# Which PSUM bank the score products for the row maxima of a causal attention use, and in which order they come

## The chip, the cores and the metric

One Trainium2 chip, of which the kernel uses one core. Times are device microseconds (us) of that core. TensorE is called PE, its weight loads PEld, VectorE DVE, ScalarE ACT, GpSimd POOL, SyncE SP, as in the profile. A bank is one eighth of the core's PSUM, as wide as 512 float32 numbers on each of 128 partitions; the kernel holds one matmul result in one.

## The reference

A diffusion transformer block with adaptive layer norm, in float32, for x of 2 x 2048 x 512 and a condition of 2 x 512:

```python
mod = silu(condition) @ Wada + bada
sh_a, sc_a, gt_a, sh_m, sc_m, gt_m = split(mod, 6)
xm = layernorm(x, g1, be1) * (1 + sc_a) + sh_a
x = x + gt_a * attention(xm, Wqkv, Wproj, bproj)   # 16 heads of 32, causal softmax
xm = layernorm(x, g2, be2) * (1 + sc_m) + sh_m
x = x + gt_m * (gelu(xm @ W1 + b1) @ W2 + b2)      # 512 -> 2048 -> 512
```

The part that matters is `attention`: for each head, scores of 2048 queries with the keys up to their own place, softmax over the keys, and the weighted sum of the values. The softmax subtracts each query's largest score, so this maximum has to be known before the exponentials are taken.

## The kernel before, in words

**Stages.** QKV of batch 0 (to 209 us), attention of batch 0 (209 to 741), projection and QKV of batch 1 (to 981), attention of batch 1 (981 to 1516), projection and the MLP (to the end, 2338). The attention of both batches runs the same program with the same order.

**Units and steps.** A unit (`units`) is a group c of 4 heads and a block i of 512 queries: 16 units in a batch, u0 to u15, with i in the order 0, 1, 2, 3 for the first group and 0, 2, 1, 3 for the others. A unit has 4i + 3 steps (`steps_of`): 4i + 1 with a full tile of 128 keys against 512 queries, then a step with two tiles of the diagonal (384 + 128 wide) and one with the last tile (256 wide). A batch has 144 steps; steps are numbered here through the batch.

**One step** (`scores_t`). Four banks `st` are taken from a pool of four. PE first writes the negative row maxima into each, as a product of `fold` with `sel`; then, for each of four heads, the scores are added (`st<-qst,kst`). ACT takes the exponential into `e` (L630); on the diagonal POOL zeroes what lies above it (`affine_select`, L636). POOL adds the exponentials of four steps into `ee` (L658; DVE does so in the last unit). Two steps later PE multiplies the exponentials with the values (`o`) and the sums with ones (`sm`).

**The maxima of later units** are found beside this, with the same scores computed a second time, the other way round (queries on partitions): "score products", `s<-kst,qst` in the trace. Their list is `Row.todo`, filled by `banks_of`: an item fills one bank, and is a unit, a key block and one or two parts (head, row tile). For a key block before the diagonal an item is a *single*: 128 queries against 512 keys, without a mask. In the diagonal block a row tile t needs only 128(t + 1) keys; tiles of 128 and 384, or of 256 and 256, go together as a *pair* in one bank, and the tile of 512 is a masked single. A unit has 6 pairs and 4 + 16i singles, 10 + 16i banks; a batch 544. `bank` issues the products and, for each part, DVE's maximum: `tensor_reduce` (L500) without a mask, and with a mask a custom operation that writes `junk`, with a read of its accumulator (both L495).

After a unit's last item, `split` (L503 to L521: operations at L517, L518, L519, L520 and L521) writes the maximum as three bfloat16 pieces into `mhl`; two of its intermediate results lie in the PSUM bank of that last item. Later `rows` transposes `mhl` on PE (`ps_m`) and DVE builds `fold` from it (L565).

**Banks.** PSUM's eight banks in the attention: `st` four, `o` and `sm` one each, and `s` two, for score products and for `ps_m`. One score product of each step with three or more of them borrows an st bank (`st_bank`), so such a step takes five banks from the pool of four: the fourth `fold` product of the next step goes into the bank in which the borrowed score product was. In the last unit, the fifth and sixth of every six st allocations go to the s pool instead.

**Order.** `count` and `due` decide how many items a step issues (n, by costs, so that each unit's maxima are ready some steps ahead). Within a step their places are fixed: one after the first head, one after the second, both in s banks; at the end a third in the borrowed bank and a fourth in an s bank, before the `o` products of an earlier step. Items are taken strictly in the list's order. PE, ACT and POOL run in the program's order; DVE's maxima, splits and folds are placed by a scheduler. During QKV, `tick` calls `score` for the first three units, without borrowing.

Of the kernel before, what the change touches and what calls it, by code (L numbers as in the profile page):

```python
# [27 lines left out]
def dit_block_kernel(  # L28
# [42 lines left out]
    HC = P // HD  # L71
# [63 lines left out]
    first = const.tile([P, 1], F32, tag="first", name="first")  # L135
# [68 lines left out]
    def mm(*args, **kw):  # L204

        return tc.keep_in_program_order(nc.tensor.matmul(*args, **kw))  # L206

    def act(ins):

        return tc.keep_in_program_order(ins)  # L210
# [84 lines left out]
    class Row:  # L295
# [234 lines left out]
                n += 1  # L530
            return n

        def score(self, n, borrow=None):

            for k in range(n):
                if borrow and k % 2 == 0:
                    s = borrow()  # L540
                else:
                    s = ps_sp.tile([P, QB], F32, tag="s", name="s")
                item = self.todo.pop(0)
                u = item[0]
                if self.mx is None:
                    self.mx = bp.tile(
                        [P, HC * TQ, units[u][1] + 1], F32, tag="mx", name="mx", bufs=3
                    )
                self.bank(*item, s)
                if not self.todo or self.todo[0][0] != u:  # L550
                    self.split(u, self.mx, s)
                    self.mx = None
                    self.at += 1
# [26 lines left out]
    def attention_phase(row):  # L580
        b, vv, kst, qst = row.b, row.vv, row.kst, row.qst
        with pool(f"att{b}") as ap, pool(
# [6 lines left out]
            def scores_t(u, step, n):  # L589

                def st_bank():

                    n_bank[0] += u == len(units) - 1
                    if n_bank[0] % 6 >= HC:
                        return ps_sp.tile([P, QB], F32, tag="s", name="st")
                    return ps_stp.tile([P, QB], F32, tag="st", name="st")

                c, i = units[u]
                tiles = steps_of[u][step]
                q0 = tiles[0][1]
                w = sum(QB - q for _, q in tiles)
                sts, es = [], []  # L610
                for h in range(HC):
                    g = slice(h * HD, (h + 1) * HD)
                    st = st_bank()
                    mm(
                        st[:, :w], sel[g, :], fold[u % 2][g, q0 : q0 + w],
                        start=True, stop=False,
                    )
                    sts.append(st)
                for h in range(HC):
                    at = 0  # L620
                    for j, q in tiles:
                        mm(
                            sts[h][:, at : at + QB - q],
                            kst[c, j // TQ][:, h, j % TQ * P : (j % TQ + 1) * P],
                            qst[u][:, h, q:],
                            start=False, stop=at + QB - q == w,
                        )
                        at += QB - q
                    e = ap.tile([P, QB], F32, tag="e", name="e", bufs=E_BUFS)
                    act(nc.scalar.activation(e[:, :w], sts[h][:, :w], AF.Exp))  # L630
                    if tiles[0][0] >= i * TQ:

                        d = e.rearrange("p (t k) -> p t k", k=P)[:, 0 : TQ : TQ - 1, :]
                        d = d[:, : len(tiles), :]
                        act(
                            nc.gpsimd.affine_select(  # L636
                                d, d, pattern=[[0, len(tiles)], [1, P]],
                                compare_op=ALU.is_ge, fill=0.0,
                                base=0, channel_multiplier=-1,
                            )  # L640
                        )
                    es.append(e)
                    if h < 2 and n >= 3 or h >= HC - n and n < 3:
                        row.score(1)
                if n >= 3:
                    row.score(1, st_bank)
                    row.score(min(n, HC) - 3)
                return es, max(0, n - HC)

            def new_sums():  # L650
# [59 lines left out]
            def due(u, step):  # L710

                rate, past = 0.0, weight[step]
                for v in range(u + 1, len(units)):

                    left = sum(weight[step : max(step + 1, starts[v] - 3)])
                    rate = max(rate, (cum[v] - row.spent) / left)
                return row.spent + rate * past

            for u, (c, i) in enumerate(units):
# [5 lines left out]
                for n_step, tiles in enumerate(steps_of[u]):  # L725
                    last = n_step == steps - 1
                    if n_step == 0:
# [5 lines left out]
                    n = row.count(  # L733
                        due(u, starts[u] + n_step) - QB // 2,
                        u + AHEAD - (n_step < 2 and u > 0),
                    )
                    if u == 0 and n_step < LAG:

                        n = max(n, HC)
                    es, rest = scores_t(u, n_step, n)  # L740
                    rest = len(row.todo) - rest
                    make_rows = False
# [37 lines left out]
                    if n_step < i * TQ:  # L780
                        k = n_step % TQ
# [492 lines left out]
    row = Row(0)  # L1274
# [167 lines left out]
    past, row = row, Row(1)  # L1442
# [594 lines left out]
```

## Time and profile before

| | |
|---|---|
| median of 3 runs | 2343.66 us (2343.58 to 2346.75) |
| profiled execution | 2339.57 us, span 2337.8, granted clock 0.997 |
| POOL's additions (L658, into a running sum) | 424 of 1293 ns |
| exponentials (L630) | 1152 of 578 ns |
| score products in s banks / in st banks (matmuls) | 994 / 286 |
| full-width maxima from s / from st banks (L500) | 608 / 160 |
| splits in s / in st banks | 24 / 8 |

The table counts operations in the whole program, with both batches. A row of the profile names engine, line, operation and `out<-in` tiles with the shape; the times in a timeline row are start and duration, and in brackets stands how long the engine was idle ahead of it and what released it. PE's matmuls are pipelined: their starts are recorded, their ends are modelled, so that rows overlap.

### The profile page before, as it was taken

The page shows a single profiled execution, that of the slowest core. Times are in us where ns is not written, and L with a number is a line of the kernel's source. Part 1 is how long each engine was busy: PE and PEld are TensorE (multiplying, and loading weights), DVE is VectorE, ACT ScalarE, POOL GpSimd, SP SyncE. Part 2 cuts the span into 40 slices and gives each one's busy share as a digit, 9 for nine tenths or more (in the row PEclk, how much of TensorE's full clock was granted, in tenths as well). Part 3 has the DMA queues.
Part 4 walks back from the last instruction along what each step waited for, and adds up shares of the span by engine and source line. Part 5 has one row for each costly group of instructions (what it writes and reads, how often), then busy time and mean ns, then how long its engine had stood idle before and what let it go on. Part 6 is the DMA issues. An engine that isn't in the chain of part 4 may idle for free.

```text
span 2337.8 us, 34364 instructions
## 1 busy us (share of the span) xinstructions
PE 2272.5 (97%) x12033; PEld 1376.1 (59%) x12033; DVE 1432.3 (61%) x3025; ACT 1007.9 (43%) x1952; POOL 1119.2 (48%) x1261
## 2 busy tenths in 40 slices
PE   7999999999999999999999999999999999999998
PEld 5787445455544588754545554344585486487477
DVE  4677766767657657777576766562473383375356
ACT  4434555555555243355555555603323322332320
POOL 7153997988893692289888898450000000000000
PEclk9999999999999999999999999999999999999999
DMA  9887132231223796622324113263354254353433
GB/s 303 272 277 185 33 86 65 64 83 46 91 100 116 260 307 222 167 60 67 75 64 100 42 42 133 97 229 108 107 176 154 84 176 145 116 162 126 141 120 131
DMA packets 160518, 311.64 MB, mean 133 GB/s; under 512 B 16544, under 2 KB 48844, under 8 KB 158552
## 3 DMA queue, kind: packets, MB, share of 16 engines
q1 hardware_dynamic: 155488, 285.53, 40.5%
q0 software_dynamic: 4480, 23.36, 2.6%
q8 instruction: 95, 1.56, 0.3%
q14 instruction: 79, 0.65, 0.1%
q10 hardware_dynamic: 376, 0.55, 0.1%
HBM read 229.95 MB, written 87.29 MB: 136 GB/s over the span
## 4 chain that ended last, share of the span: by engine, by line
PE 83%; DVE 6%; POOL 6%; issue 2%; DMA 2%; ACT 1%; SPq 0%; DVEq 0%; POOLq 0%; ACTq 0%
PE ps_a L206 24%; PE st L206 15%; PE ps_b L206 12%; PE o L206 9%; PE s L206 7%; PE ps_c L206 6%; POOL ee L658 5%; PE sm L206 4%; PE ps_o L206 3%; DVE junk L495 2%; PE ps_xt L214 1%; DVE mx L500 1%; POOL e L636 1%; ACT e L630 1%; PE ps_o L214 1%
## 5 line engine op out<-in xcount | busy, mean ns | idle before, releaser
L630 ACT ACTIVATE e<-st 128x512 f32<-128x512 f32 (+1 forms) x1152 | 574.5, 578 | 413.6 <-PE st L206 380.0
L500 DVE TENSOR_REDUCE mx<-s 128x1 f32<-128x512 f32 x608 | 406.2, 686 | 223.1 <-PE s L206 221.8
L658 POOL TENSOR_TENSOR ee<-ee,e 128x512 f32<-128x512 f32 x424 | 529.1, 1293 | 3.5 <-ACT e L630 3.3
L206 PE MATMUL st<-qst,kst 128*128 128x512 f32 (+3 forms) x1280 | 410.6, 386 | 0.0
L206 PE MATMUL s<-kst,qst 128*128 128x512 f32 (+3 forms) x994 | 375.3, 402 | 6.0 <-DVE mx L500 3.1
L206 PE MATMUL ps_a<-sum,w 128*128 128x256 f32 (+1 forms) x1088 | 346.6, 454 | 0.0
L206 PE MATMUL o<-e,vv 128*32 128x512 f32 (+3 forms) x2560 | 310.2, 539 | 6.9 <-POOL e L636 6.7
L206 PEld LDWEIGHTS st<-qst,kst 128*128 128x128 f32 x1280 | 227.8, 188 | 117.6 <-issue 88.3
L206 PEld LDWEIGHTS ps_a<-sum,w 128*128 128x128 f32 x1088 | 206.4, 190 | 109.7 <-issue 91.3
L658 POOL TENSOR_TENSOR ee<-e 128x512 f32<-128x512 f32 x168 | 210.3, 1288 | 102.3 <-ACT e L630 100.6
L495 DVE CUSTOM_DVE_ANT_0 junk<-s,causal 128x128 bf16<-128x128 f32 (+3 forms) x386 | 188.5, 488 | 92.4 <-PE s L206 85.0
L206 PEld LDWEIGHTS s<-kst,qst 128*128 128x128 f32 x994 | 185.7, 188 | 55.5 <-DVE mx L500 20.5
L636 POOL TENSOR_SCALAR_AFFINE_SELECT e<-e 128x128 f32<-128x128 f32 (+1 forms) x384 | 123.6, 362 | 73.1 <-ACT e L630 70.8
L206 PEld LDWEIGHTS <-sel 32*128 32x128 bf16 x1152 | 29.5, 91 | 199.7 <-issue 199.7
L1616 DVE TENSOR_TENSOR h<-c,ps_b 128x512 f32<-128x512 f32 x32 | 22.0, 688 | 202.0 <-PE ps_b L206 202.0
L206 PE MATMUL st<-fold,sel 32*128 32x512 bf16 (+1 forms) x1152 | 127.9, 372 | 13.5 <-DVE mx L495 6.4
L206 PEld LDWEIGHTS o<-e,vv 128*32 128x32 f32 x2560 | 65.3, 108 | 112.4 <-issue 72.8
L1790 ACT ACTIVATE h<-h,cols 128x512 f32<-128x512 f32 x96 | 69.3, 722 | 120.5 <-DVE h L1616 120.5
L206 PE MATMUL ps_b<-sum,w 128*128 128x256 f32 (+1 forms) x384 | 120.6, 450 | 0.0
L500 DVE TENSOR_REDUCE mx<-st 128x1 f32<-128x512 f32 x160 | 109.4, 684 | 2.4 <-PE st L206 0.6
L985 POOL TENSOR_TENSOR lo<-lo,hi 128x512 fp32r<-128x512 f32 x32 | 40.7, 1274 | 130.4 <-ACT hi L983 124.1
L206 PE MATMUL st<-kst,qst 128*128 128x512 f32 (+3 forms) x286 | 98.0, 370 | 0.0
(210 smaller groups left out, 3113.9 us busy)
## 6 DMA issues: line engine op xcount, KB each, us to landing
kst<-k SPq DMA_DIRECT2D x128, 256.0 KB
qst<-q SPq DMA_DIRECT2D x128, 256.0 KB
w<-w1d SPq DMA_DIRECT2D x32, 896.0 KB
w<-w2d SPq DMA_DIRECT2D x28, 1024.0 KB
w<-w2d SPq DMA_DIRECT2D x28, 768.0 KB
q<-hi SPq DMA_DIRECT2D x32, 256.0 KB
q<-lo SPq DMA_DIRECT2D x32, 256.0 KB
k<-hi SPq DMA_DIRECT2D x32, 256.0 KB
```

Source lines behind the costliest of these rows:

```text
L206: return tc.keep_in_program_order(nc.tensor.matmul(*args, **kw))
L214: return tc.keep_in_program_order(nc.tensor.transpose(dst, src, ident[:n, :n]))
L495: nc.vector.tensor_tensor_reduce(junk[:, :w], x, causal[:, QB - w :], 1.0, MASKED, ALU.add, ALU.max, m,)
L500: nc.vector.tensor_reduce(m, x, axis=AX.X, op=ALU.max)
L630: act(nc.scalar.activation(e[:, :w], sts[h][:, :w], AF.Exp))
L636: nc.gpsimd.affine_select(d, d, pattern=[[0, len(tiles)], [1, P]], compare_op=ALU.is_ge, fill=0.0, base=0, channel_multiplier=-1,)
L658: act(engine.tensor_tensor(dst, x, y, ALU.add))
L985: engine.tensor_tensor(lo, d, hi.bitcast(F32), ALU.subtract)
L1616: act(nc.vector.tensor_tensor(dst, x, y, ALU.add))
L1790: nc.scalar.activation(d, ps, AF.Gelu, bias=col(r_b1 + half * HF + f, 1))
```

## The change

`score` gets a third argument, and looks ahead over the first eight items of the list that belong to the unit whose turn it is. Items with two parts are `pairs`, the others `singles`. The borrowed bank is taken only if a single is among them and the unit's last item isn't the only one left (the item after which `split` runs in the item's bank); else the product goes to an s bank. The item taken is the first single of those ahead, and for the call at the end of a step (`late=True`) the first pair; where there is none of the kind, the first item. The order within a unit thus changes; which items belong to which unit does not, nor how many a step issues, but for the costs that `count` finds in the items that are left.

```diff
-        def score(self, n, borrow=None):
+        def score(self, n, borrow=None, late=False):
             for k in range(n):
-                if borrow and k % 2 == 0:
+                u = self.todo[0][0]
+                ahead = [j for j, item in enumerate(self.todo[:8]) if item[0] == u]
+                pairs = [j for j in ahead if len(self.todo[j][2]) > 1]
+                singles = [j for j in ahead if j not in pairs]
+                lent = borrow and singles and len(ahead) > 1
+                if lent:
                     s = borrow()
                 else:
                     s = ps_sp.tile([P, QB], F32, tag="s", name="s")
-                item = self.todo.pop(0)
-                u = item[0]
+                first = pairs if late else singles
+                item = self.todo.pop((first or [0])[0])
...
                 if n >= 3:
                     row.score(1, st_bank)
-                    row.score(min(n, HC) - 3)
+                    row.score(min(n, HC) - 3, late=True)
```

The calls during QKV (`late` not given) take singles first too. After the change, lines behind L533 stand five lines further down.

## The prediction

> **What bounds the kernel now.** First the page: which engine is busy, and which engines stand on the chain that ends last.
>
> ```profile
> PE 2272.5 (97%) x12033; PEld 1376.1 (59%) x12033; DVE 1432.3 (61%) x3025; ACT 1007.9 (43%) x1952; POOL 1119.2 (48%) x1261
> PE 83%; DVE 6%; POOL 6%; issue 2%; DMA 2%; ACT 1%; SPq 0%; DVEq 0%; POOLq 0%; ACTq 0%
> ```
>
> TensorE (PE) is the bound, and the change leaves it the same matmuls. So only time in which PE is held can be won or lost. Next, the waits of PE over the whole span (us in total, times, longest), as far as they end on buffers of the attention:
>
> ```profile
> PE o L206 <- POOL e L636: 6.7, 10, 1.2
> PE st L206 <- DVE mx L495: 6.4, 12, 0.8
> PE st L206 <- DVE mhl L521: 6.2, 8, 1.1
> PE s L206 <- DVE mx L500: 3.1, 6, 1.1
> PE s L206 <- DVE mhl L521: 1.8, 4, 0.6
> ```
>
> The second and third rows are what the diff can touch first. A step opens with four `st<-fold` products into the four st banks; the borrowed bank makes a fifth allocation in a step, so the fourth fold product of the next step waits until VectorE (DVE) has read the borrowed bank. The timeline of PE shows five such steps, an unheld one (407.03), and an s product that waits for a split (276.81):
>
> ```profile
> 265.04 0.39 PE L206 MATMUL st<-fold,sel 32*128 32x512 bf16 x3
> 266.14 0.37 PE L206 MATMUL st<-fold,sel 32*128 32x512 bf16 x1 [0.70 <-DVE mx L495]
> ...
> 276.81 0.50 PE L206 MATMUL s<-kst,qst 128*128 128x512 f32 x1 [0.62 <-DVE mhl L521]
> ...
> 289.29 0.65 PE L206 MATMUL st<-fold,sel 32*128 32x512 bf16 x4
> ...
> 407.03 0.40 PE L206 MATMUL st<-fold,sel 32*128 32x512 bf16 x4
> ...
> 410.45 0.39 PE L206 MATMUL st<-fold,sel 32*128 32x512 bf16 x3
> 411.65 0.37 PE L206 MATMUL st<-fold,sel 32*128 32x512 bf16 x1 [0.81 <-DVE mhl L521]
> ...
> 414.92 0.39 PE L206 MATMUL st<-fold,sel 32*128 32x512 bf16 x3
> 416.06 0.37 PE L206 MATMUL st<-fold,sel 32*128 32x512 bf16 x1 [0.75 <-DVE mx L495]
> ...
> 685.57 0.39 PE L206 MATMUL st<-fold,sel 32*128 32x512 bf16 x3
> 686.60 0.37 PE L206 MATMUL st<-fold,sel 32*128 32x512 bf16 x1 [0.64 <-DVE mhl L521]
> ```
>
> Unheld, four such products take 0.40 in one row (407.03): they start almost together. In the first pair of rows the fourth starts 1.10 after the first: PE lost 1.09, although only 0.70 is shown as idle, since the drawn ends of the first three cover the rest. At 289.29 no idle time is shown and the row is 0.65 long: 0.28 lost. Read in this way, from starts, batch 0 has 25 held steps, the first that at 265.04, the last that at 685.57, 14.1 us together, and batch 1 repeats them: 28.1 us in all, of which 17.6 end on the maxima of masked products (L495), 9.3 on the last operation of the split (L521), and 1.2 on L500. The first two, **26.9 us**, are what the edit aims at.
>
> The shown idle time gives 6.4 + 6.2 = 12.6 instead. [...]
>
> What holds the bank is seen on DVE, ahead of 266.14:
>
> ```profile
> 264.93 0.82 DVE L565 TENSOR_TENSOR fold<-ps_m,tmask 128x640 bf16<-128x640 bf16 x1
> 265.66 0.41 DVE L495 CUSTOM_DVE_ANT_0 junk<-st,causal 128x256 bf16<-128x256 f32 x1
> ```
>
> and in a split, which starts at its first row and frees its bank after its last:
>
> ```profile
> 316.27 0.20 DVE L517 TENSOR_REDUCE st<-mx 128x16 f32<-128x48 f32 x1
> 317.06 0.19 DVE L521 TENSOR_TENSOR mhl<-st,mhl 128x16 bf16<-128x16 f32 x1
> ```
>
> So a split holds its bank for 0.98 us (316.27 to 317.25). The cost of a pair against a single comes from these rows of DVE:
>
> ```profile
> 199.53 0.42 DVE L495 CUSTOM_DVE_ANT_0 junk<-s,causal 128x256 bf16<-128x256 f32 x1
> ...
> 200.51 0.69 DVE L500 TENSOR_REDUCE mx<-s 128x1 f32<-128x512 f32 x1
> ...
> 313.86 1.29 DVE L500 TENSOR_REDUCE mx<-s 128x1 f32<-128x512 f32 x2 [0.89 <-PE s L206]
> ```
>
> A pair occupies DVE for 0.98 from its start to the next operation (0.93 to 1.05 by what follows); two full-width reductions take 1.29 with 0.69 for the second, so one step of the queue is 0.60. A pair is about 0.35 dearer, which is the size of the many small holds of 0.28 to 0.35. [...]
>
> **The change, part by part.** The order of instructions of the two programs has the same operations on every engine, and PE, ACT, POOL and SP keep theirs apart from which score product stands at which place. These rows, by shape and by tile, give what is moved:
>
> ```profile
> L206 PE MATMUL st<-fold,sel 32*128 32x512 bf16 x1024 | 117.4, 384 | 13.1 <-DVE mx L495 6.4 <-DVE mhl L521 6.2
> L500 DVE TENSOR_REDUCE mx<-st 128x1 f32<-128x512 f32 x160 | 109.4, 684 | 2.4 <-PE st L206 0.6
> ...
> L495 DVE CUSTOM_DVE_ANT_0 junk<-st,causal x126: 280/547/693, 264.6 to 1458.8; 128x128 bf16<-128x128 f32 x34, 128x384 bf16<-128x384 f32 x34, 128x512 bf16<-128x512 f32 x30, 128x256 bf16<-128x256 f32 x28
> ...
> L517 DVE TENSOR_REDUCE st<-mx x8: 198/228/228, 316.3 to 1459.6; 128x16 f32<-128x64 f32 x6, 128x16 f32<-128x48 f32 x2
> ```
>
> Before, the borrowed banks hold 160 full-width unmasked singles, 30 masked full-width singles, 48 pairs (34 of 128 + 384, 14 of 256 + 256) and 8 splits. After, 190 unmasked and 36 masked singles, no pair, no split. So the edit does what it says, and the holds that end on pairs and splits go. Where no single is left, the pair goes to an s bank, of which there are two, and all 32 splits run in s banks. What is late next I follow stretch by stretch, queueing the new order of products on the two s banks and on DVE with the durations above. Per batch:
>
> - *End of unit 2 (steps 14 to 17, 265 to 277 us).* Before: 1.09, 0.73 and 0.74 at the fourth fold, and 0.78 at 276.81 where an s product waits for a split: 3.34. After: steps 15 and 16 are `single, pair, pair` and `pair, pair, pair`, all in s banks; I find 0.06 at a fold, 0.43 at an s bank in step 16, and 1.5 in step 17, where the late pair waits for a reduction that stands behind the split: 2.0 (bounds 0.5 without that wait, 3.3 as before). Gain **1.3**.
> - *Steps 20 to 22.* Two borrowed pairs become singles: 0.28 + 0.32 held before, 0.1 after. Gain **0.5**.
> - *Step 27/28 (316.1).* The split leaves the st bank: 1.16 before, 0.1 after. POOL follows closely here (below). Gain **1.0**.
> - *Ends of units 6 and 10 (steps 52 to 55, 88 to 91).* Before 1.20 + 1.14 at folds, 0.29 and 0.28 beside: 2.9 each. After, DVE has, in four steps, 7 pairs at 1.05 (7.4), 7 singles at 0.6 to 0.8 (4.4), two splits at 0.98 (2.0) and one L565 of 0.82: 14.6 us, against 13.5 of PE (four steps of 3.3 to 3.4: 407.03 to 410.45 is 3.42, 410.45 to 414.92 is 3.27 without its hold). The excess is 1; with the places where DVE has to wait for a product, I find PE held about 2.2 (bounds 1.0, and 2.9 as before). Gain **0.7** each, 1.4.
> - *Step 109, and the transpose ahead of it.* A borrowed pair goes; 0.35 + 0.37 held. Gain **0.7**. *Start of unit 14*: **0.2**.
> - *The other holds, late in units 3, 5, 7, 9, 11, 13 and 14, 4.1 us in all.* **Nothing.** Their cover is POOL:
>
> ```profile
> 347.81 0.87 PE L206 MATMUL o<-e,vv 128*32 128x384 f32 x3 [0.95 <-POOL e L636]
> ...
> 326.52 2.52 POOL L658 TENSOR_TENSOR ee<-e 128x512 f32<-128x512 f32 x2 [1.00 <-ACT e L630]
> ...
> 431.62 2.52 POOL L658 TENSOR_TENSOR ee<-e 128x512 f32<-128x512 f32 x2 [4.60 <-ACT e L630]
> ...
> 410.45:414.92 4.47, 3.66 (x26) 1.84 (x23) 3.13 (x15) 2.06 (x4) 4.47 (x5) 1.00 0.01 4
> ```
>
> The last row is a window: PE busy 3.66, DVE 3.13, POOL 4.47 of 4.47 us. Within a unit POOL works without a pause from its first addition on, and at the unit's end the `o` products wait for its select. A hold taken away behind that point makes PE wait longer at `o`, as at 347.81. A hold ahead of a pause of POOL (1.00 before 326.52, 4.60 before 431.62) is won as far as the pause reaches. If POOL were not in the way, these 4.1 us would be won too.
>
> - *Added cost.* In step 0 and 1 a pair stands next to the transpose that shares the s banks: **−0.3**. In the QKV stage (scores between projections) six pairs come in a row at the ends of units 0, 1 and 2, 1.05 us of DVE each beside a 0.42 addition, where products come every 1.1 to 1.2 us. PE there waits for DVE's additions today only so much:
>
> ```profile
> PE ps_a L206 <- DVE vv L1053: 2.1, 2, 1.5
> ```
>
> That row is the stretch from 0 to 209 us. What the clusters add isn't shown; I bound it by 0 (the queue of two banks takes it up) and −1.0 per batch (three clusters, each late by one 0.35), and take **−0.4**, nearer to 0 as the row is short.
>
> Sum per batch: 1.3 + 0.5 + 1.0 + 1.4 + 0.7 + 0.2 − 0.3 − 0.4 = 4.4; for two batches 8.8, or **about 9 us**. The profiled execution took 2339.57 us (span 2337.8 and 1.8 around it), 4.1 below the median of 2343.66, so the difference is put on the median: 2343.66 − 8.8 = 2334.9, **2335 us** (−0.4%).
>
> **The rivals.**
>
> *All of it is won.* If neither POOL nor the crowded unit ends hold PE, the gain is the 26.9 us less the share late in units (2 × 4.1 = 8.2): 18.7, so **2325 us**. For it: DVE is busy 61% of the span, with room on average. Against it: the ends of units 2, 6 and 10 need more of DVE than PE gives them time.
>
> *Moved, not removed.* The holds at the fourth fold reappear at the s banks and at `o`. If the residues at the ends of units 2, 6 and 10 are as large as what was there, and POOL eats step 28 as well, there remain per batch 0.5 + 0.7 + 0.2 − 0.7 = 0.7: 2 × 0.7 = 1.4, **2342 us**, no change that can be measured. For it: an s product that waits holds PE just as a fold product does, as the row of L500 (3.1 us, 6 times) shows. [...]
>
> *Slower: the crowded s banks.* With only pairs left, every product of a step waits in one of two banks for a pair two places ahead, at 1.05 us each, and a split of 0.98 in the same pool comes on top. It decides if the residues that I put at 2.0 (unit 2) and 2 × 2.2 (units 6, 10) are more than 6.4 + 4.4 = 10.8 per batch. At twice my figure, 12.8, and −1.0 in the QKV stage, a batch loses 6.4 + 0.6 − 4.4 = 2.6: **2349 us**. Against it: DVE's work in those four steps is beyond PE's by 1 us, not 4.
>
> *That the change doesn't do what it says* is excluded by the order of instructions.
>
> **How the numbers follow.** About 0.2% (4.7 us) is what a measurement of this kernel can tell from no change: faster means under 2339.0, slower over 2348.3. The forecast has 0.50 (2330 to 2340), all won 0.12, moved 0.24, slower 0.14. From the first, 0.47 lies beyond the bound; with all won 0.59 faster; same 0.27; slower 0.14. The range reaches from 2325 (all won) to 2347, most of the way to the slower case.
>
> **What would show it.** In the changed kernel's waits of PE, `st` held by L521 is gone, and `st` held by L495 is near zero (only masked singles remain). `s` held by L500, L495 and L521 rises from 5 us to some 10, around 270 to 277 and 410 to 424 us. `o` held by POOL's select rises by up to 8 us, at 347 and 697. The attention stages, 209 to 741 and 981 to 1516, shrink by about 4 to 5 us each; the QKV stage grows by less than 1. The forecast is wrong if `o` takes up the gain of step 28 or of units 6 and 10 (POOL has less room than its pauses say), or if waits at `s` come in every step of the unit ends.

## The result, and the profile after

| | before | changed |
|---|---|---|
| median of 15 runs | 2343.58 us (2339.29 to 2346.80) | 2336.67 us (2332.27 to 2343.72) |
| ratio | 1 | 0.9972, 95% interval 0.9963 to 0.9980 |
| profiled execution's span | 2337.8 us, clock 0.997 | 2333.8 us, clock 0.995 |
| first fold product of the attention, batch 0 | 208.67 us | 213.82 us |
| attention, batch 0 (first fold product of step 0 to that of step 143) | 527.75 us | 524.52 us |
| attention, batch 1 | 529.73 us | 523.96 us |

The kernel is 6.9 us faster by the medians, where 8.8 was forecast. In the two attention stages of the profiled executions it is 3.2 and 5.8 faster. The stretch ahead of them is 5.15 us longer in this execution. Some 2 us of it are there before the first score product is issued (73.00 us before, 75.06 after), and so don't come from the change: the windows of the first 30 us show another granted clock (the number after POOL's count), 1.00 before and 0.89 after.

Before:

```profile
0.00:30.00 30.00, 18.12 (x73) 10.71 (x74) 16.96 (x47) 12.65 (x21) 16.94 (x33) 1.00 0.87 290
```

After:

```profile
0.00:32.30 32.30, 20.87 (x65) 10.43 (x65) 17.98 (x45) 10.75 (x17) 18.25 (x34) 0.89 0.77 260
```

The rest, some 3 us, comes in two places. The later one (1.5 us, at 133 us of the kernel before) is shown below to be the change's. At the earlier one (1.9 us, at 124 us) an s product of the changed kernel waits 1.46 us for a masked maximum; it does so, for 1.4 to 2.2 us, in all five kernels with the new order in QKV, while in the other nine it waits there for something else or not at all, 0 to 1.7 us. How much of this is the change's is open. Over the executions profiled for this study the attention begins between 207.0 and 210.9 us in the nine kernels that keep the list's order during QKV, and between 210.4 and 214.7 in the five that don't. So the stages are compared below by their own lengths, and QKV by itself.

Engines, chain and waits of PE after the change:

```profile
PE 2272.0 (97%) x12033; PEld 1385.7 (59%) x12033; DVE 1435.1 (61%) x3025; ACT 1008.4 (43%) x1952; POOL 1121.3 (48%) x1261
PE 86%; POOL 4%; DVE 4%; DMA 2%; issue 2%; ACT 1%; SPq 0%; POOLq 0%; DVEq 0%; ACTq 0%
```

```profile
PE o L206 <- POOL e L641: 12.1, 8, 2.4
...
PE s L206 <- DVE mx L500: 6.0, 10, 1.2
...
PE s L206 <- DVE mx L495: 3.9, 9, 1.5
...
PE st L206 <- DVE mx L495: 1.7, 4, 0.4
...
PE s L206 <- DVE mhl L521: 0.6, 2, 0.3
```

Fold products wait 1.7 us in place of 12.6, and for no split any more. The s banks hold PE for 10.5 us in place of 4.9. And `o` waits for POOL's select 12.1 us in place of 6.7, in fewer and longer waits: up to 2.4 us. Four of these are new in kind. Here are the two of batch 0 in PE's timeline; the rows of before are 347.81 (2.13 us for 16 products after 0.95 idle, partly shown in the prediction) and 697.23:

```profile
350.09 3.00 PE L206 MATMUL o<-e,vv 128*32 128x384 f32 x16 [2.37 <-POOL e L641]
353.01 0.61 PE L206 MATMUL st<-fold,sel 32*128 32x512 bf16 x4
...
697.70 3.00 PE L206 MATMUL o<-e,vv 128*32 128x384 f32 x16 [2.25 <-POOL e L641]
700.63 0.61 PE L206 MATMUL st<-fold,sel 32*128 32x512 bf16 x4
```

From before's timeline:

```profile
697.23 2.13 PE L206 MATMUL o<-e,vv 128*32 128x384 f32 x16 [1.20 <-POOL e L636]
699.29 0.40 PE L206 MATMUL st<-fold,sel 32*128 32x512 bf16 x4
```

The same 16 products and the way to the next fold take 2.06 us in the kernel before (697.23 to 699.29) and 2.93 in the changed one (697.70 to 700.63). The windows around the wait tell why; the third number from the end is the granted clock:

```profile
695.40:697.70 2.30, 0.04 (x2) 0.00 (x1) 0.00 (x0) 1.50 (x4) 2.30 (x4) 1.00 0.24 94
697.70:699.00 1.30, 1.30 (x9) 0.63 (x13) 0.00 (x0) 0.00 (x0) 1.30 (x5) 0.87 0.00 0
699.00:700.60 1.60, 1.60 (x13) 0.50 (x4) 0.00 (x0) 0.00 (x0) 0.73 (x3) 0.50 0.00 0
700.60:702.70 2.10, 2.10 (x10) 1.14 (x9) 0.00 (x0) 0.61 (x2) 0.00 (x0) 0.65 0.00 0
```

PE stood still for 2.25 us, POOL was busy all of that time, and after it TensorE's granted clock fell to half for 3.4 us. The fall did not come with the end of the wait at 697.70 but at 698.65. Windows cut at the places where the clock changed, and one such length ahead, show this:

```profile
695.24:698.65 3.41, 1.16 (x6) 0.41 (x6) 0.00 (x0) 1.67 (x4) 3.41 (x7) 1.00 0.17 68
698.65:702.07 3.42, 3.42 (x19) 1.63 (x17) 0.00 (x0) 0.00 (x0) 1.08 (x5) 0.50 0.00 0
702.07:705.48 3.41, 3.41 (x47) 1.43 (x46) 2.50 (x4) 2.35 (x5) 0.00 (x0) 1.00 0.00 0
```

In each of the fourteen traces, all changes of the granted clock lie whole multiples of 3.413 us apart; in the changed kernel's these are, in the attentions, 350.49, 353.91, 698.65, 702.07, 1118.49, 1121.90, 1466.65 and 1470.06. Places one such length apart are called marks here. A mark at which the clock doesn't change is an estimate, counted on from a change in the same trace. Where the marks fall differs from one execution to the next: one lies at 695.24 in the changed kernel and at 696.33 in the kernel before. This matters for the experiments on the clock below.

Unit by unit, batch 0, from the starts of the first fold products (batch 1 repeats these within 0.4 us, but for unit 0 of four kernels with the list's order, told at the end):

| units | before | changed | splits only | rule only | order only | changed + DVE | order + DVE | before + DVE |
|---|---|---|---|---|---|---|---|---|
| 0 and 1 | 37.19 | 36.87 | 37.19 | 37.19 | 36.85 | 36.86 | 36.87 | 37.19 |
| 2 | 43.43 | 42.62 | 43.43 | 42.33 | 43.68 | 42.61 | 43.66 | 43.42 |
| 3 | 56.00 | 52.84 | 55.36 | 55.38 | 52.89 | 53.37 | 53.37 | 61.31 |
| 4 | 12.48 | 15.13 | 12.44 | 12.79 | 13.80 | 10.90 | 10.91 | 10.96 |
| 5 and 9 | 78.60 | 79.33 | 78.66 | 80.20 | 79.23 | 79.33 | 79.25 | 78.65 |
| 6 and 10 | 59.00 | 56.18 | 57.49 | 56.05 | 57.34 | 56.07 | 57.31 | 59.23 |
| 7 and 11 | 110.68 | 109.87 | 110.73 | 112.44 | 109.86 | 109.93 | 109.89 | 110.69 |
| 8 and 12 | 24.17 | 23.90 | 24.10 | 24.13 | 24.83 | 23.81 | 24.87 | 24.13 |
| 13 | 39.05 | 38.95 | 39.09 | 39.86 | 38.92 | 38.96 | 38.92 | 39.06 |
| 14 | 25.24 | 24.42 | 24.29 | 23.50 | 25.30 | 24.38 | 25.26 | 25.21 |
| 15, to its last step | 41.92 | 44.42 | 42.80 | 42.83 | 41.98 | 39.62 | 39.58 | 39.56 |

Unit 3 wins 3.2 us and unit 4 gives 2.65 of it back; unit 14 wins 0.8 and unit 15 gives back 2.5. These two places make the question of the experiments.

### The profile page after: what moved, and what is told of

The parts are those of the page before. It is cut to its first block, busy times and chain, and to the rows that moved or that the text cites. A ratio compares the mean times of both kernels' runs of the same rounds, so it can differ in the third digit from the quotient of the medians.

```text
span 2333.8 us, 34344 instructions
## 1 busy us (share of the span) xinstructions
PE 2272.0 (97%) x12033; PEld 1385.7 (59%) x12033; DVE 1435.1 (61%) x3025; ACT 1008.4 (43%) x1952; POOL 1121.3 (48%) x1261
## 4 chain that ended last, share of the span: by engine, by line
PE 86%; POOL 4%; DVE 4%; DMA 2%; issue 2%; ACT 1%; SPq 0%; POOLq 0%; DVEq 0%; ACTq 0%
PE ps_a L206 24%; PE st L206 16%; PE ps_b L206 12%; PE o L206 10%; PE s L206 8%; PE ps_c L206 6%; PE sm L206 4%; POOL ee L663 3%; PE ps_o L206 2%; DVE junk L495 2%; PE ps_xt L214 1%; DVE mx L500 1%; PE ps_o L214 1%; ACT e L635 1%; DMA q<-hi 1%
## 5 line engine op out<-in xcount | busy, mean ns | idle before, releaser
L500 DVE TENSOR_REDUCE mx<-s 128x1 f32<-128x512 f32 x578 | 381.5, 686 | 232.0 <-PE s L206 231.0
L206 PE MATMUL s<-kst,qst 128*128 128x512 f32 (+3 forms) x1054 | 381.0, 393 | 10.7 <-DVE mx L500 6.0
L206 PE MATMUL o<-e,vv 128*32 128x512 f32 (+3 forms) x2560 | 314.5, 543 | 12.1 <-POOL e L641 12.1
L495 DVE CUSTOM_DVE_ANT_0 junk<-s,causal 128x128 bf16<-128x128 f32 (+3 forms) x476 | 224.9, 472 | 65.9 <-PE s L206 52.1
L206 PEld LDWEIGHTS s<-kst,qst 128*128 128x128 f32 x1054 | 196.0, 188 | 70.8 <-DVE mx L500 21.7
L500 DVE TENSOR_REDUCE mx<-st 128x1 f32<-128x512 f32 x190 | 129.6, 682 | 0.4
L206 PE MATMUL st<-fold,sel 32*128 32x512 bf16 (+1 forms) x1152 | 117.5, 375 | 2.8 <-DVE mx L495 1.7
L206 PEld LDWEIGHTS ps_b<-sum,w 128*128 128x128 f32 x384 | 73.0, 190 | 37.2 <-issue 30.6
```

The source lines that it names most:

```text
L495: nc.vector.tensor_tensor_reduce(junk[:, :w], x, causal[:, QB - w :], 1.0, MASKED, ALU.add, ALU.max, m,)
L500: nc.vector.tensor_reduce(m, x, axis=AX.X, op=ALU.max)
```

## The experiments

**Theory A:** the change takes the holds away, but ahead of the ends of units 3 and 14 POOL is what PE runs into; the wait there grows past a length at which the clock falls as well. **Theory B:** the holds count for themselves, and what grew elsewhere has other causes.

### Parts of the change alone

The code in this part and the next is shown as differences from the changed kernel, but for `before + DVE`; "..." stands for further lines.

`splits only`: pairs may be borrowed, the list's order is kept, and only the unit's last item, with its split, stays out of the st banks.

```diff
-                lent = borrow and singles and len(ahead) > 1
+                lent = borrow and len(ahead) > 1
...
-                first = pairs if late else singles
-                item = self.todo.pop((first or [0])[0])
+                item = self.todo.pop(0)
```

> Of the edit, only this: the unit's last item isn't put in a borrowed bank, so that the split leaves the st banks; pairs may still be borrowed, and items keep the list's order. Theory A (the holds removed are won only where POOL has room; where it has none, PE's wait for POOL's select at the end of units 3 and 14 grows past 2 us, and the granted clock then falls to 0.5 for some 3 us, about 1.3 us lost each time): the splits of units 5 to 7 and 9 to 11 are won (2 x 2 x 1.2 = 4.8 us), those ahead of units 4 and 15 are not, and cost the clock's 1.3 up to four times: 2341 to 2344. Theory B (each hold counts for itself): all 9.3 us are won, 2334.

2339.46 us, ratio 0.9979 (0.9967 to 0.9991): 4.9 less, between the two. As A has it, the split of unit 14 is won there (0.95) and given back in unit 15 (0.9). But the clock did not fall: the row and the windows behind it show 2.11 us idle, 2.13 for the 16 products, and 1.00.

```profile
693.40 2.13 PE L206 MATMUL o<-e,vv 128*32 128x384 f32 x16 [2.11 <-POOL e L640]
```

```profile
693.40:695.50 2.10, 2.10 (x20) 0.86 (x20) 0.00 (x0) 0.00 (x0) 2.01 (x7) 1.00 0.01 3
695.50:699.00 3.50, 3.50 (x41) 1.75 (x44) 1.97 (x4) 2.06 (x4) 0.00 (x0) 1.00 0.00 0
```

A wait of 2.11 us was not enough here, and 2.25 was in the changed kernel. But the two differ in more than their length. By the changes of the clock in its trace, this execution has a mark at 691.95, which cuts the wait into 0.67 and 1.45 us, so PE stood still for no more than 1.45 us between two marks:

```profile
688.54:691.95 3.41, 2.74 (x19) 1.02 (x17) 0.00 (x0) 2.49 (x7) 3.41 (x4) 1.00 0.14 40
691.95:695.36 3.41, 1.96 (x16) 0.82 (x16) 0.00 (x0) 0.79 (x2) 3.41 (x9) 1.00 0.10 40
```

In the changed kernel the whole 2.25 us lay between two marks. This run also decides how holds are counted: the one at 685.57 in before was 1.03 by starts and 0.64 by shown idle time, and its removal won 0.95 in unit 14.

`rule only`: a borrowed bank only for a single that is next in the list.

```diff
-                lent = borrow and singles and len(ahead) > 1
+                lent = borrow and 0 in singles and len(ahead) > 1
...
-                first = pairs if late else singles
-                item = self.todo.pop((first or [0])[0])
+                item = self.todo.pop(0)
```

> The borrowing rule alone: a borrowed bank only if the next item of the list is a single and not the unit's last; the order of the list is kept. Theory A: no fold product is held by a pair or a split any more, the same two waits for POOL as in the changed kernel (2.2 to 2.4 us with the clock at 0.5), and pairs in the third place now crowd the s banks: half of the change's gain, 2339 to 2341. Theory B (only the holds at the fold count, the order of items does nothing): as the changed kernel, 2336 to 2337.

2342.41 us, ratio 0.9995 (0.9986 to 1.0004): no difference that can be told, and less than either theory had. The fall of the clock that A had at both places came at neither: the waits at `o` are 1.25 us at unit 4 and 2.11 at unit 15, and the 16 products behind each take 2.13 us, as in the kernel before. Units 2, 6, 10 and 14 win 1.1 to 1.7 us each; units 5, 7, 9, 11 and 13 lose 0.6 to 1.1 each, because a pair in the third place now stands in an s bank ahead of the fourth. In the waits that is a row which the kernel before doesn't have for a masked maximum (stretch of batch 0), the transposes waiting for their s bank:

```profile
PE ps_m L565 <- DVE mx L495: 2.7, 6, 0.5
```

`order only`: singles first, a pair last, and every third product borrowed whatever it is.

```diff
-                lent = borrow and singles and len(ahead) > 1
+                lent = borrow
```

> The order alone: singles first, a pair last in a step, but every third product of a step is borrowed, as before. Theory A: the many holds of 0.3 us go, those of 1.1 at the ends of units 2, 6 and 10 stay, where only pairs are left, and with them the splits that fall on a borrowed bank: 2339 to 2342, with s waits of under 4 us. Theory B (the borrowing rule is what counts): within 1 us of the kernel before, 2343.

2336.94 us, ratio 0.9971 (0.9959 to 0.9982): all of the change's gain, more than either theory had. It looks as if the borrowing rule were worth nothing. The table says otherwise: with the rule, units 2, 6 and 10, 8 and 12, and 14 are 1.1, 1.2, 0.9 and 0.9 shorter, 4.0 per batch (6 and 10, and 8 and 12, taken together), and units 4 and 15 are 1.3 and 2.4 longer. The 1.3 is chance in part or whole: the wait at unit 4 is 2.26 us here and 2.37 in the changed kernel, but a mark cuts it into 1.35 and 0.92, and the clock stayed at 1.00.

### POOL out of the way

In units 3 and 14 the four additions of the step before the diagonal go to VectorE, which has hardly any maxima left there:

```diff
-            def add(u, h, dst, x, y):
-                engine = nc.vector if u == len(units) - 1 else nc.gpsimd
+            def add(u, h, dst, x, y, by_dve=False):
+                by_dve = by_dve or u == len(units) - 1
+                engine = nc.vector if by_dve else nc.gpsimd
...
-                        add_to(u, chain, es)
+                        add_to(u, chain, es, HC if u in (3, len(units) - 2) else 0)
```

`changed + DVE`:

> The changed kernel, and in units 3 and 14 the four additions of the step before the diagonal are made by VectorE in place of POOL. Theory A: POOL reaches its selects 5 us earlier, the four waits of 2.2 to 2.4 us go and with them the clock's fall: 4 x (2.3 + 1.3) = 14 us less than the changed kernel, less what the additions cost on VectorE, 2323 to 2327; granted clock 1.00 at the ends of units 3 and 14. Theory B (the long waits are another form of the removed holds and something else comes late at once): 2333 to 2337.

2319.21 us, ratio 0.9893 (0.9879 to 0.9906): 17.5 below the changed kernel, more than A's 14. The long waits are gone from the list, and the clock stays at 1.00 (windows of the ends of units 3 and 14):

```profile
PE o L206 <- POOL e L641: 2.7, 4, 0.7
```

```profile
346.00:352.00 6.00, 5.88 (x46) 2.80 (x44) 1.96 (x3) 3.74 (x10) 4.93 (x13) 1.00 0.68 159
690.00:696.00 6.00, 6.00 (x52) 2.45 (x56) 4.99 (x7) 4.77 (x12) 3.15 (x7) 1.00 0.02 3
```

The attention stages take 515.84 and 516.07 us, 8.7 and 7.9 less than in the changed kernel, 16.6 together: units 3 and 4 make 3.7 and unit 15 4.8 per batch.

`order + DVE` (the order alone, with the same additions on VectorE):

> The order alone (every third product borrowed, as before), with the four additions of units 3 and 14 on VectorE. Theory A (the borrowing rule does remove holds at the ends of units 2, 6, 8, 10 and 14, but POOL ate them): per batch 1.0 in unit 2, 0.6 each in units 6 and 10, 0.9 each in units 8 and 14 more than with the rule: 2319 + 8 = 2327. Theory B (the borrowing rule is worth nothing, as the run with the order alone has it without VectorE's additions): 2319 to 2321.

2329.84 us, ratio 0.9941 (0.9928 to 0.9953): 10.6 above `changed + DVE`, where A had 8. The attention stages make 4.1 and 3.8 of it, which is A's 8; the rest lies outside them. The borrowing rule is worth about 8 us in the attention, and in the changed kernel POOL and the clock took that back.

`before + DVE`:

> The kernel before, with the same four additions of units 3 and 14 on VectorE. Theory A (POOL eats what the change wins late in units 3 and 14): the waits of 0.95 and 1.20 us in each batch go, and nothing else: 2 x 2.15 = 4.3 us less, 2338 to 2340, so that the change would be worth some 19 us with POOL out of the way and 7 without. Theory B (the additions on VectorE are a gain of their own, whatever the order of the products): as much as with the change, 17 us, 2326.

2348.47 us, ratio 1.0020 (1.0009 to 1.0031): slower, which neither theory had. Units 4 and 15 win more than A said (1.5 and 2.4, where it had 0.95 and 1.20), but unit 3 loses 5.3. PE's row and DVE's rows there:

```profile
344.95 0.58 PE L206 MATMUL st<-fold,sel 32*128 32x512 bf16 x1 [3.37 <-DVE mx L495]
```

```profile
341.11 0.08 DVE L495 DVE_READ_ACCUMULATOR2_ANT mx<- 128x1 f32 x1
343.16 1.26 DVE L659 TENSOR_TENSOR ee<-ee,e 128x512 f32<-128x512 f32 x1 [1.96 <-POOL e L636]
344.34 0.55 DVE L495 CUSTOM_DVE_ANT_0 junk<-st,causal 128x384 bf16<-128x384 f32 x1
```

An addition that waits 1.96 us for POOL was queued on DVE between the two halves of a borrowed pair, and the fourth fold product waited 3.37 us for the second half; behind that the clock was 0.50:

```profile
344.90:348.00 3.10, 3.05 (x10) 2.42 (x9) 1.80 (x3) 1.65 (x4) 0.81 (x2) 0.50 0.00 0
```

The attention stages lose 1.7 and 1.3 us. The profiled execution was the slowest of the twelve (2356.32 us, 2340.88 to 2356.32), and 12 us more than before lie between its two attentions; how much of that comes from the edit is not shown. So the same edit wins nothing in the kernel before, 7.1 us with the new order, and 17.5 with the new order and the borrowing rule.

### How long a wait lowers the clock

The kernel before, with POOL's select for the first head of the two-tile step repeated in units 3 and 14, two or four times more (against the kernel before):

```diff
-                        act(
-                            nc.gpsimd.affine_select(
...
+                        again = 2 if u in (3, len(units) - 2) and h == 0 and len(tiles) > 1 else 0
+                        for _ in range(1 + again):
+                            act(
+                                nc.gpsimd.affine_select(
...
```

> The kernel before, but POOL's select of the first head in the two-tile step of units 3 and 14 is made three times in place of once (the further ones change nothing in the result). PE's waits for it grow by 2 x 0.36 us, to about 1.7 and 1.9. Theory A (PE's clock falls only after a longer wait, above 2.1 us): granted clock 1.00 behind both, the 16 products take 2.13 us. Theory B (the clock falls in proportion to any wait, or for another reason than the wait): below 1.00 behind the wait at unit 14.

One run of 2349.47 us. The four waits are 1.92, 2.16, 1.62 and 2.17 us, and their row and windows part: after 1.92 the clock is 1.00, after 2.16 it falls to 0.50. That fits A's "above 2.1 us", but A's case of some 1.9 at unit 15 was not met, since that wait came out longer. Nor does it show a length: a mark cuts the 1.92 into 1.52 and 0.39 and the 1.62 into 1.18 and 0.44, while 2.16 and 2.17 each lie whole between two marks.

```profile
350.97 1.23 PE L206 MATMUL o<-e,vv 128*32 128x384 f32 x5 [1.92 <-POOL e L638]
...
701.31 0.87 PE L206 MATMUL o<-e,vv 128*32 128x384 f32 x3 [2.16 <-POOL e L638]
```

```profile
351.00:353.00 2.00, 2.00 (x16) 0.79 (x16) 0.00 (x0) 0.00 (x0) 2.00 (x8) 1.00 1.06 230
...
701.30:703.40 2.10, 2.09 (x13) 1.15 (x15) 0.00 (x0) 0.00 (x0) 2.02 (x7) 0.70 0.01 4
703.40:705.50 2.10, 2.10 (x12) 0.92 (x9) 0.00 (x0) 0.00 (x0) 0.00 (x0) 0.50 0.00 0
```

> As before, with that select made five times: waits of about 2.4 and 2.6 us. Theory A: the clock falls to 0.5 behind all four waits, the 16 products take 2.9 to 3.0 us, and the stretch to the second fold after it gets some 1.3 us longer than the wait explains. Theory B (in the changed kernel something else lowers the clock, such as the crowded products ahead of it): 2.13 us, granted clock 1.00.

One run of 2358.56 us, waits of 2.87, 3.15, 2.58 and 3.14 us, and the clock falls behind all of them. Behind the first it is at 0.50 over the whole 2.9 us of the products:

```profile
352.70:355.60 2.90, 2.88 (x16) 1.60 (x16) 0.00 (x0) 0.00 (x0) 2.90 (x11) 0.50 1.07 215
```

The crowded products of the changed kernel aren't needed for the fall: the kernel before has it too, once the wait is made longer.

By length alone the waits of all these runs don't part well: 2.27 us (`order only`, unit 4) did not lower the clock, 2.16 (unit 15 here) did. The longest piece of a wait between two marks parts them better:

| waits at `o` | longest piece between two marks, us | clock after it |
|---|---|---|
| changed kernel, four waits | 2.37, 2.25, 2.04, 2.25 | 0.50 |
| select three times, unit 15 of both batches | 2.16, 2.17 | 0.50 |
| select five times, four waits | 2.79, 2.12, 1.61, 3.14 | 0.50 |
| select three times, unit 4 of both batches | 1.52, 1.18 | 1.00 |
| `splits only`, unit 15 of both batches | 1.45, 1.35 | 1.00 |
| `rule only`, unit 15 of both batches | 1.14, 1.99 | 1.00 |
| `order only`, unit 4 of both batches | 1.35, 1.29 | 1.00 |

The marks are worked out from the clock's changes in each trace. A piece of 1.61 with a fall and one of 1.99 without show that something else counts as well. No run moved the marks on purpose, so this is read from the traces, not tested.

### QKV, and the crowded ends of units

`list QKV + DVE`: `changed + DVE`, but with the list's order until the attention of the batch begins.

```diff
+            self.attends = False
...
-                first = pairs if late else singles
+                first = pairs if late else singles if self.attends else []
...
+            row.attends = True
...
```

> The changed kernel with VectorE's additions in units 3 and 14, but during the QKV stage items keep the list's order (no pairs in a row at the ends of units 0 to 2). Theory A: the new order costs 1.5 us in the QKV of batch 0, in the stretch that in the kernel before lies between 130 and 135 us, and nothing in batch 1: that stretch is as before, and the time 1 to 2 us less than with the new order, 2318. Theory B (the clusters cost nothing that a run shows, the stretch differs by chance): 2319, and the stretch 1.5 longer than before here too.

2316.50 us, ratio 0.9881 (0.9864 to 0.9897), **the fastest kernel of the study**, 2.7 below `changed + DVE`, where A had 1 to 2. PE's rows of the stretch in question, from the condition's transposes to the end of the next token transposes, first in the changed kernel (132.76 to 140.62, 7.86 us):

```profile
132.76 0.95 PE L206 MATMUL ps_modt<-pickc,mr 128*128 128x4 f32 x8
138.94 0.33 PE L214 MATMUL ps_xt<-ident,x 128*128 128x128 f32 x1 [0.56 <-ACT x L897]
139.64 0.98 PE L214 MATMUL ps_xt<-ident,x 128*128 128x128 f32 x7 [0.38 <-ACT x L897]
```

and in this one (129.62 to 136.00, 6.38; the kernel before has 128.89 to 135.26, 6.37):

```profile
129.62 0.95 PE L206 MATMUL ps_modt<-pickc,mr 128*128 128x4 f32 x8
134.96 1.04 PE L214 MATMUL ps_xt<-ident,x 128*128 128x128 f32 x8
```

The new order costs 1.5 us in this stretch, of which the two waits of PE's transposes for ACT make 0.9; that it is the pairs in a row that put ACT off was not shown, nor what makes the other 1.2 of the 2.7.

`mixed + DVE`: where more pairs than singles lie ahead, s banks take pairs early.

```diff
-                first = pairs if late else singles
+                many = len(pairs) > len(singles) and not lent
+                first = pairs if late or many else singles
```

> The changed kernel with VectorE's additions, but where more pairs than singles lie ahead, a place in an s bank takes a pair (the borrowed bank still a single): in the units with i = 0 pairs and singles are mixed instead of four singles and then six pairs. Theory A (the crowded s banks at the ends of units 2, 6 and 10 hold PE because pairs stand in a row): of the 1.2 us at unit 2 and 1.5 each at units 6 and 10 two thirds go, 2319 - 5.5 = 2314. Theory B (VectorE has too much to do there in any order, as its sum of work says): within 1.5 us of 2319.

2325.26 us, ratio 0.9924 (0.9908 to 0.9940): 6.0 slower than `changed + DVE`, outside both theories. Mixing the pairs in is not the remedy that A took it for. The attention is 3.0 longer in each batch, in units 2, 6, 8, 10 and 12. The holds at the fold come back, now because the borrowed masked single waits on DVE behind two pairs:

```profile
412.79 0.37 PE L206 MATMUL st<-fold,sel 32*128 32x512 bf16 x1 [0.77 <-DVE mx L495]
```

`list QKV + mixed + DVE`, both edits:

> Both: the list's order in the QKV stage, and pairs mixed in the units with i = 0. If both theories A hold, the sum of the two gains: 2312 to 2313; if neither does, 2319.

2323.72 us, ratio 0.9914 (0.9896 to 0.9932): the loss of the mixing with the gain in QKV.

`list QKV + wide + DVE`: the look-ahead goes over the rest of the unit.

```diff
-                ahead = [j for j, item in enumerate(self.todo[:8]) if item[0] == u]
+                ahead = [j for j, item in enumerate(self.todo[:80]) if item[0] == u]
```

> As the run with the list's order in QKV and VectorE's additions, but score looks over the whole rest of the unit in place of the first eight items, so that a unit's six pairs go last in six steps in a row and its end has singles only (but for units with i = 0, whose ends stay crowded). Theory A (what is left of the holds sits at the ends of the units with i = 0, which this doesn't touch): within 2 us of 2316.5. Theory B (pairs that fall near each other in the other units still hold PE at the s banks, 0.2 to 0.3 us each): 4 us less, 2312.

2323.31 us, ratio 0.9912 (0.9898 to 0.9926): slower than with eight items, outside both theories. The attention stages are 1.2 and 2.5 longer, 2.0 of the second in unit 0 of batch 1. In both batches a late pair stands in step 1 ahead of the transpose, and the next s product waits longer than the 1.07 to 1.08 us of all other kernels:

```profile
981.95 0.50 PE L206 MATMUL s<-kst,qst 128*128 128x512 f32 x1 [1.55 <-DVE fold L571]
```

In batch 1 this wait lies whole between two marks (979.80 and 983.21) and the clock is at 0.50 for the next 3.4 us; in batch 0 it is cut, the clock stays at 1.00, and unit 0 loses 0.4. So some 1.5 of the 2.0 go with the clock. The other 3 us lie outside the attention and may be chance.

## Why the prediction was right, step by step

**The bound, and how holds are counted.** Right: PE's work stayed the same, and its holds moved the time. Counting from starts was the better reading (0.95 won where 1.03 by starts and 0.64 by idle time was held).

**Unit 2 (1.3).** 0.8 and 0.95. The wait that was forecast at 1.5 in step 17 is there, as 1.17 us for a reduction (L500).

**Steps 20 to 28 (0.5 + 1.0).** The mechanism was right, the account incomplete. Units 3 and 4 together won 0.5 us: 3.2 in unit 3, and 2.65 back. POOL's pauses of 0.37 and 1.00 us ahead of 310.58 and 326.52 are gone; in the changed kernel POOL goes on without one (318.82 + 9.99 ends behind the next start):

```profile
313.85 5.02 POOL L663 TENSOR_TENSOR ee<-e 128x512 f32<-128x512 f32 x4
318.82 9.99 POOL L663 TENSOR_TENSOR ee<-ee,e 128x512 f32<-128x512 f32 x8
328.75 3.80 POOL L663 TENSOR_TENSOR ee<-e 128x512 f32<-128x512 f32 x3
```

So what PE won was kept as far as the pauses reached, as forecast. The rest went into the wait for the select, from 0.95 to 2.37. What the prediction did not have is the clock: 0.86 us on the 16 products and 0.36 on the following step, 1.2 in all.

**Units 6 and 10 (0.7 each).** 1.4 each: the term was mis-sized. What is left there is one hold of 0.8 by starts and s waits of 0.2 to 0.4, 1.4 together, where 2.2 was forecast. The forecast took the order of DVE's queue as harder than it was. `mixed + DVE`, which spreads the pairs and loses, fits DVE being the limit there, but does not show it, since it also brought holds at the fold back.

**Unit 12 and the start of unit 14 (0.7 and 0.2).** 0.5 in unit 12; unit 14 0.8, but that holds the split of step 126, which unit 15 gave back.

**The late holds, "nothing".** They were worth less than nothing. In unit 15 the wait grew by 1.05 (1.20 to 2.25), which is the hold taken away, and the clock's fall came on top with 1.5 us (0.87 on the products, 0.62 in the step that follows). With the 1.2 of unit 4 this is 2.7 per batch, **5.4 us** that no step of the prediction had. This is the profiled execution, in which all four waits had 2.04 us or more between two marks. Over the fifteen executions the granted clock goes from 0.996 (five of the seven fastest) to 0.992 (the slowest), so other executions can have fewer or more such falls.

**The added cost (0.3 and 0.4 per batch).** Units 0 and 1 won 0.3 in place of losing it. QKV lost 1.5 or more in batch 0 (0.4 was forecast) and nothing in batch 1 that stands out from chance (the stretch between the attentions took 244.3 us before and 244.2 after).

**The sum.** Without QKV it said 9.6 us; the attention stages won 9.0. But two misses stand against each other in this: the clock's 5.4, and on the other side units 6 and 10 (2.8), units 0 and 1 (1.2), and 1.7 us of unit 0 in batch 1. That last one was not foreseen either: in the kernel before, the clock fell behind the wait of 1.07 at 988.17.

```profile
989.00:991.00 2.00, 1.89 (x7) 1.22 (x7) 1.80 (x6) 1.09 (x4) 0.58 (x2) 0.72 1.08 224
991.00:993.00 2.00, 2.00 (x13) 0.51 (x16) 0.81 (x2) 0.30 (x2) 0.57 (x2) 0.50 1.11 227
```

That these misses nearly cancel is luck: the sum came out close, while its terms for units 6 and 10, for the late holds and for QKV did not.

**The rivals.** "All of it is won" (18.7) was out of reach while POOL paced the ends of units 3 and 14; `changed + DVE` passes it (25 us below the kernel before), with the earlier waits for POOL gone too. "Moved, not removed" holds for units 4 and 15. The crowded s banks did not decide: s waits rose by 5.6 us in all, as the forecast (to some 10) had it.

## What to carry to other kernels

When a stall is taken away ahead of a stage that another engine paces, look at how long the next wait becomes, not only at whether the gain survives: here a wait of about 1 us that grew to 2.3 cost 1.2 us (unit 4) and 1.5 us (unit 15) more than its length, because the clock fell to 0.50 behind it. Whether it fell went with where the clock's marks lay (behind the wait of 1.55 us in `list QKV + wide + DVE` it was 0.50 in one batch and 1.00 in the other), so two profiles are no ground for a limit on the length of a wait. The borrowing rule showed no gain when it was tried alone, and the additions on VectorE a loss; added together to the new order they are worth 17.7 us (2336.94 to 2319.21), so a part that shows no gain alone should be tried again once the next limit is out of the way. And the order of an engine's queue is part of the move: in `before + DVE` an addition put on VectorE landed ahead of the maximum that held a bank, and a fold product waited 3.37 us.

## What the runs showed of the hardware

- TensorE's granted clock was 1.00 or 0.50 in the records of these traces, and its 136 changes in the fourteen traces lay on marks that were 3.4133 us apart within each execution (to 0.005 us). A fall behind a wait of PE came at the mark that cut the wait (at 1118.49 in the changed kernel, for the wait from 1116.45 to 1118.81) or at the next one after it (at 989.88 in the kernel before, 1.7 us behind the end of the wait at 988.17), at most 2.1 us behind its end (`before + DVE`, batch 1). The clock was back at 1.00 one mark later, after 3.41 us (behind all four waits at `o` of the changed kernel), or two, after 6.83 us (behind the wait of 3.37 us in `before + DVE`).
- In the attentions and between them (205 to 1530 us), each of the 20 pieces of a wait that lasted 2.0 us or more between two marks was followed by 0.50 (nine of them, 2.04 to 3.14 us, stand in the table above); of the 19 pieces of 1.5 to 2.0 us, 6 were. A wait of 2.67 us between the attentions of the kernel before (903.06 to 905.73), which a mark cuts into 1.48 and 1.19, was followed by 1.00.
- A wait of 1.07 us in step 1 of a batch was followed by a fall to 0.50 (the windows of the kernel before, above) in batch 1 of four of the six kernels that keep the list's order, and in batch 0 of a fifth. In these six kernels it lay whole between two marks six times, and five of them brought the fall; it was cut by a mark six times, and none did. In the seven kernels that take the new order there with eight items ahead, a wait just as long lay whole five times and never brought it. What the new order changes there stays open.
- An addition of 128x512 float32 numbers took 0.78 us on VectorE (mean of 72 in `changed + DVE`) where it took 1.29 on POOL (mean of 424 in the kernel before):

```profile
L664 DVE TENSOR_TENSOR ee<-ee,e 128x512 f32<-128x512 f32 x72 | 51.8, 780 | 13.1 <-POOL e L641 9.6 <-ACT e L635 3.5
```
